# A four-layer recurrent kernel: zero rows in the head stacks, and turns for POOL's indirect transfers

## The chip, the cores and the metric

The kernel runs on one core of a Trainium2 chip. The metric is the device time of one execution in microseconds (us), and less is better. One program does everything, from the inputs in DRAM to the output in DRAM. The engines are called PE (TensorE; PEld is its weight load), DVE (VectorE), ACT (ScalarE), POOL (GpSimd) and SP (SyncE). SP computes nothing here, and issues transfers.

## The reference

`x` is `[2, 1024, 128]`, 2048 tokens of 128 numbers. Four times a layer normalisation gives `xn`, a first block gives `s` and a second one `g`:

```python
for each of four layers:
    xn = layernorm(x)
    s  = block_a(xn)
    g  = silu(block_b(xn))
    x  = x + s * g
```

Layer 0 is a differential attention with 8 heads of 2 x 128 and a feed-forward part with ternary weights. Layer 2 is a "quantum circuit" (cosines and their cumulative products) and a mixture of 16 experts that choose tokens. The change touches what serves layers 1 and 3:

```python
# layer 1, first block: 16 heads of 8 numbers, each token sees 32 to either side
scores = einsum('bhqd,bhkd->bhqk', Q, K) / sqrt(8)
scores = where(abs(i - j) <= 32, scores, -inf)
s = einsum(softmax(scores), V) @ W_o
# layer 1, second block: every token goes to one of 8 experts (the top one)
top_idx = argmax(softmax(x @ gate_w.T)); top_val = max(...) / (max(...) + 1e-8)
out = (gelu(x @ w1[top_idx]) @ w2[top_idx]) * top_val
out = layernorm(out) * ln_gamma + ln_beta
# layer 3, first block: 16 heads of 8 numbers, causal; second block: int4 weights and LoRA
```

## The kernel before, in words

The tokens are 16 tiles of 128. Each layer is a function of its own, and the layers follow each other in time: layer 0 up to about 1030 us, layer 1 from 1035 to 1350, layer 2 to 1645, layer 3 to the end.

The class `Heads` serves the attention of layers 1 and 3. `project_in` makes queries and keys, and `split3` writes each number as a sum of three bf16 parts. The parts go to DRAM (`parts`, L522), and `load_stacks` (L546, L552) brings them back as two stacks for four heads: `kk[n % 3]` (called ks in the profile) and `q[n % 3]` (qs), each `[KR, 4, S]`. Rows 0 to 71 hold products' factors, nine blocks of 8 rows, so that one bf16 matmul over 72 rows adds up all products of parts. Row maxima come first: `maxima` multiplies rows `0:KP` (72) and DVE takes the maximum (nm, L958). The negated maxima, in three bf16 parts, are then transposed and written to rows `KP:KR` (72 to 74) of qs by `maxima_rows`, where ks has ones (L491, three POOL transfers). The scores (st, L976) multiply rows `0:KR` (75), so that the maximum is subtracted inside the matmul, ACT takes the exponential (e, L1012), and `values` (o1p, L623) multiplies with v. Masks are added by a matmul of the identity with a mask in SBUF (L938, L967). A group n is four heads of one batch entry: eight groups a layer. The stacks of group n + 2 are loaded while group n is worked on, all of them from SP.

The experts of layer 1 are the class `Routed`. `route` (L649) computes each token's expert and place, and ends with 16 indirect transfers on POOL (`slots_in<-xn`, L729) that scatter the tokens into DRAM sorted by expert, 128 slots to a tile, 23 tiles (`NS1`). `steps` (L737) is a generator: per tile one indirect load of the expert's weights (`ew`, L763), which POOL issues two steps ahead, a transpose and two matmuls (L772 on), and after eight tiles the gelu and the second matmuls (`f1y`). The tokens' rows (`xs`, L748) come in three SP loads of up to 8 tiles. At the end 16 indirect loads (L835) bring the results back, one in each step, and a layer normalisation per four tiles follows.

The order of the work is written out by hand: `manual_schedule` keeps the program's order on PE, DVE, ACT and POOL. `Weave` runs two generators beside each other, here `attend(n, o)` (16 steps) and `ahead(n)`, which holds the maxima of group n + 1 and `MOE[n]` steps of the experts:

```python
MOE = (2, 8, 11, 11, 11, 11, 12, 16)
```

77 steps are to be done, and the last places of `MOE` give out a few more than are left. SP's queue has its own order, which the framework's planner makes; a transfer waits there for the eighth one before it of its kind of queue. In the first 60 us SP also writes zeros into the 23 tiles of slots (L1819) and later issues transposed tiles of layer 0 (`aT<-tT`, L292).

Of the kernel before, what the change touches and what calls it, by code (L numbers as in the profile page):

```python
# [2 lines left out]

# [1 line left out]

# [5 lines left out]
F32 = mybir.dt.float32  # L11
BF16 = mybir.dt.bfloat16
# [6 lines left out]
P = 128  # L19
B, S, D = 2, 1024, 128  # L20
NT = B * S // P
NG = NT // 4
# [7 lines left out]
E1, FF1 = 8, 256  # L30
NS1 = NT + E1 - 1
# [37 lines left out]
def rsqrt(k, pool, out, in_, n):  # L69

    k.nc.gpsimd.tensor_tensor(out, in_, k.neg_half[:, :n], ALU.pow)  # L71
# [379 lines left out]

KP, KR = 72, 75


class Heads:
# [5 lines left out]
    def __init__(self, k, ctx, weave, li, qk, v, o, bq=None, bk=None, bv=None, bo=None):  # L463
        nc, tc = k.nc, k.tc
        self.k, self.weave, self.li = k, weave, li
        self.wqk = k.wm(qk).rearrange("p (a c) -> p a c", a=2)
        self.wv, self.wo = k.wm(v), k.wm(o)
        self.bk, self.bv, self.bo = bk, bv, bo

        def pool(name, bufs, **kw):  # L470
            return ctx.enter_context(tc.tile_pool(name=f"a{li}{name}", bufs=bufs, **kw))

        self.big, self.fx, self.wk, self.ep, self.sp = (pool(n, c) for n, c in (("b", 1), ("x", 2), ("w", 2), ("e", 5 if li == 1 else 8), ("s", 3)))
        self.dr = pool("d", 1, space=bass.MemoryType.DRAM)
        self.p_s, self.p_t, self.p_o = (pool("p" + n, c, space=PSUM) for n, c in (("s", 3), ("t", 3), ("o", 2)))

        self.ident_h = self.big.tile([P, P], BF16, tag="ident_h", name=f"ident_h{li}")
        nc.vector.tensor_copy(self.ident_h, k.ident)

        self.v = self.big.tile([P, NT, H1 * self.VW + 32], F32, tag="v", name=f"v{li}")  # L480
        nc.gpsimd.memset(self.v, 1.0)
        self.scale = 1.0 / math.sqrt(DK)
        self.bq = None
        if bq is not None:
            self.bq = self.sp.tile([P, 1], F32, tag="bq", name="bq", bufs=1)
            nc.vector.tensor_scalar(self.bq, bq, self.scale, None, ALU.mult)
        self.q, self.kk = [], []
        for j in range(3):
            self.q.append(self.big.tile([KR, 4, S], BF16, tag=f"qs{j}", name=f"qs{li}{j}"))
            t = self.big.tile([KR, 4, S], BF16, tag=f"ks{j}", name=f"ks{li}{j}")  # L490
            nc.gpsimd.dma_start(  # L491
                t[KP:KR].rearrange("p h (a t) -> p (h a) t", t=P),
                k.ones_h[0 : KR - KP, None, :].to_broadcast([KR - KP, 32, P]),
            )
# [41 lines left out]
            nc.vector.tensor_tensor(dst, src, bv, ALU.add)  # L536
        yield

    def load_stacks(self, n):

        nc = self.k.nc
        b, hg = divmod(n, 4)
        heads = slice(4 * hg, 4 * hg + 4)
        d = self.parts[b]
        for a in range(3):
            nc.sync.dma_start(  # L546
                self.kk[n % 3][24 * a : 24 * a + 24], d[1].rearrange("a (d h) t -> (a d) h t", h=H1)[:, heads, :]
            )
        for a in range(3):
            for i in range(3):  # L550
                r = 24 * a + 8 * i
                nc.sync.dma_start(  # L552
                    self.q[n % 3][r : r + DK], d[0, a].rearrange("(d h) t -> d h t", h=H1)[:, heads, :]
                )

    def maxima_rows(self, n, c, nm):

# [75 lines left out]
class Routed:  # L633
# [12 lines left out]
        for _ in range(n):  # L646
            next(self.todo, None)

    def route(self):  # L649
        k, nc, pool = self.k, self.k.nc, self.pool  # L650

        def tile(name, shape, dt=F32):
# [73 lines left out]

        self.scattered = []
        for t in range(NT):
            i = nc.gpsimd.indirect_dma_start(k.slots, self.at(self.pos, t), k.xn[:, t, :], None)  # L729
            for j in self.scattered:  # L730
                k.tc.declare_no_dep(i.ins, j.ins, reason="no two tokens have the same slot")
            self.scattered.append(i)
# [5 lines left out]
    def steps(self):  # L738
# [1 line left out]
        G = 8  # L740
        xs, h, w, late = {}, {}, {}, {}

        def first(a):


            n = min(G, NS1 - a * G)
            xs[a] = pool.tile([P, G, D], F32, tag="xs", name=f"xs{a}", bufs=2)
            d = nc.sync.dma_start(  # L748
                xs[a][:, 0:n, :], k.slots[a * G * P : (a * G + n) * P, :].rearrange("(t p) d -> p t d", p=P)
            )  # L750
            for i in self.scattered:
                k.tc.add_manual_dep(
                    d.ins,
                    i.ins.name,
                    mybir.DependencyInfo(mybir.DependencyClass.Sync, mybir.DependencyReason.DATA),
                    reason="a slot's row may come from any of the scatters",
                )

        def weights(i):

            if i < NS1:
                w[i] = hd.wk.tile([P, 2 * FF1], F32, tag="ew", name=f"ew{i}", bufs=13)
                nc.gpsimd.indirect_dma_start(w[i], None, k.i["l1_w"], self.at(self.rows, i))  # L763

        def hidden(i):

            a, j = divmod(i, G)
            if i < NS1 and j == 0:
                h[a] = pool.tile([P, 2 * G + 1, P], F32, tag="h1", name=f"h1_{a}", bufs=2)
            ph = self.p.tile([P, 3, P], F32, tag="s", name=f"f1h{i}")  # L770
            if i < NS1:
                nc.tensor.transpose(ph[:, 2, :], xs[a][:, j, :], k.ident)  # L772
            if i:
                b, l = divmod(i - 1, G)
                for c in range(2):
                    nc.tensor.matmul(
                        ph[:, c, :],
                        lhsT=w[i - 1][:, c * P : (c + 1) * P],
                        rhs=h[b][:, 2 * l, :],
                        start=True,  # L780
                        stop=True,
                    )
            if i and i < NS1 and j:
                copy_on(nc, i % 2, h[a][:, 2 * j - 2 : 2 * j + 1, :], ph)
                return
            if i:
                copy_on(nc, i % 2, h[b][:, 2 * l : 2 * l + 2, :], ph[:, 0:2, :])
            if i < NS1:
                copy_on(nc, 1 - i % 2, h[a][:, 0, :], ph[:, 2, :])
# [22 lines left out]
                k.slots_out[i0 * P : (i0 + n) * P, :].rearrange("(t p) d -> p t d", p=P), y[:, 0:n, :]  # L812
            )

        first(0)
        first(1)
        for i in range(2):
            weights(i)
        yield
        for i in range(NS1 + 8):  # L820
            if i % G == G // 2 and 2 <= (i + G) // G < (NS1 + G - 1) // G:
                first((i + G) // G)
# [8 lines left out]
            for fn in late.pop(i, ()):  # L831
                fn()
            yield
        for t in range(NT):
            nc.gpsimd.indirect_dma_start(self.y[:, t, :], None, k.slots_out, self.at(self.pos, t))  # L835
# [6 lines left out]
        for n in range(NG):  # L842
# [41 lines left out]
def l1_layer(k):  # L884
    nc, tc = k.nc, k.tc
    half = WIN // 2
    with ExitStack() as ctx:
# [4 lines left out]

        def banded(name, w, step):
            m = big.tile([P, w], BF16, tag=name, name=name)
            for r in range(0, P, step):
                part = zero[r : r + step, 0:w]
                nc.gpsimd.affine_select(
                    out=part, in_=part, compare_op=ALU.is_ge, fill=-1e30, base=0, pattern=[[1, w]], channel_multiplier=-1  # L900
                )
                nc.gpsimd.affine_select(
                    out=m[r : r + step, :],
                    in_=part,
# [3 lines left out]
                    pattern=[[-1, w]],  # L908
                    channel_multiplier=1,
                )  # L910
            return m

        zero = big.tile([P, KW], F32, tag="zero", name="zero1")
        nc.gpsimd.memset(zero, 0.0)
        band = banded("band1", KW, P)
        nc.gpsimd.memset(zero, 0.0)
        inner = banded("inner1", P, P // 2)
        first = big.tile([P, P], BF16, tag="first1", name="first1b")
        last = big.tile([P, P], BF16, tag="last1", name="last1b")
        nc.gpsimd.tensor_copy(first, inner)  # L920
# [834 lines left out]
def recurrent_kernel(ctx: ExitStack, tc, ins, out, layers=(0, 1, 2, 3)):  # L1755
# [196 lines left out]
```

## Time and profile before

| what | value |
|---|---|
| median of 3 runs | 1967.15 us (1962.88 to 1970.48) |
| the profiled execution | 2018.82 us |
| its span | 2017.1 us |
| mean granted TensorE clock in it | 0.900 |
| PE busy | 1737.7 us (86%) |
| DVE busy | 1260.8 us (63%) |
| ACT busy | 829.7 us (41%) |
| POOL busy | 554.5 us (27%) |

The profile is one execution and 51.7 us longer than the median, so a length read from it is compared with its own span. In a list of groups a line reads: code line, engine, operation, output<-inputs, rows * columns of the PE array, shape, count, then busy time, mean ns, idle time before and what ended it. PEclk in the slices of the page is the granted clock in tenths. "remote" or "another core or an unknown queue" stands where no recorded instruction explains the end of a wait, and "issue" where the engine waited for nothing that the profile shows.

### The profile page before, as it was taken

Reading aid. Unit: us, or ns where it says so; the run is one execution under the profiler, and the core shown is the slowest. Engines: PE = TensorE matmul, PEld = TensorE weight load, DVE = VectorE, ACT = ScalarE, POOL = GpSimd, SP = SyncE. Lnnn points to the kernel's source line nnn. Section 1 sums busy time; section 2 is a strip of 40 time slices with the busy share of each in tenths; the row PEclk is TensorE's granted clock in tenths of the full one; section 3 lists DMA queues with packets and bytes.
Section 4 is the critical chain, followed back from the end, with each engine's and each line's share of the span. In section 5 each row is a group of like instructions: output and inputs, shape, how many; then the busy total and the mean of one; then the engine's idle time right before and its main releaser. Section 6 shows DMA issues by size and latency. Waiting matters only on the chain.

```text
span 2017.1 us, 24516 instructions
## 1 busy us (share of the span) xinstructions
PE 1737.7 (86%) x7820; PEld 894.3 (44%) x7820; DVE 1260.8 (63%) x2561; ACT 829.7 (41%) x1803; POOL 554.5 (27%) x870
## 2 busy tenths in 40 slices
PE   4999999999999999889971888765588939999996
PEld 2444444444444444334450455433366724444442
DVE  3988888888888888830032443468732464787771
ACT  2555555555555554432140344333113131566564
POOL 2333333333333333400045012111056350111201
PEclk9999999999999999999985689775689865899998
DMA  5433233333333332400015333121045233021200
GB/s 176 104 90 101 71 96 80 97 83 97 82 83 97 81 83 71 101 3 0 0 25 143 85 102 89 36 72 41 0 111 132 46 79 72 17 65 38 47 2 12
DMA packets 115504, 141.86 MB, mean 70 GB/s; under 512 B 25923, under 2 KB 100684, under 8 KB 112816
## 3 DMA queue, kind: packets, MB, share of 16 engines
q1 hardware_dynamic: 90512, 91.94, 17.7%
q0 software_dynamic: 24576, 48.33, 10.0%
q8 instruction: 63, 1.03, 0.2%
q14 instruction: 65, 0.53, 0.1%
q10 hardware_dynamic: 288, 0.03, 0.0%
HBM read 55.76 MB, written 16.78 MB: 36 GB/s over the span
## 4 chain that ended last, share of the span: by engine, by line
PE 56%; DVE 18%; DMA 7%; issue 5%; POOL 5%; ACT 4%; SPq 2%; another core or an unknown queue 1%; POOLq 0%; DVEq 0%; ACTq 0%
PE sc L261 11%; PE pz L303 6%; PE f0h L419 5%; DVE nm L271 4%; PE o3p L623 4%; DMA aT<-tT 4%; PE st L1649 3%; PE po L321 2%; DVE e L281 2%; DVE tT L285 2%; PE pq L237 2%; SPq L292 2%; POOL aT L292 2%; PE sr L1611 2%; ACT e L273 2%
## 5 line engine op out<-in xcount | busy, mean ns | idle before, releaser
L261 PE MATMUL sc<-xnT,q 128*128 128x512 f32 x1024 | 506.3, 596 | 6.4 <-ACT e L273 6.4
L273 ACT ACTIVATE e<-sc,nm 128x1024 f32<-128x1024 f32 x256 | 285.2, 1114 | 350.1 <-DVE nm L271 267.5
L271 DVE TENSOR_REDUCE nm<-sc 128x1 f32<-128x1024 f32 x256 | 307.8, 1205 | 9.1 <-PE sc L261 9.1
L261 PEld LDWEIGHTS sc<-xnT,q 128*128 128x128 f32 x1024 | 193.8, 191 | 234.1 <-issue 189.3
L292 POOL DMA_DIRECT2D aT<-tT x384 | 204.7, 540 | 322.6 <-DVE tT L285 175.1
L303 PE MATMUL pz<-aT,xn 128*128 128x512 f32 x512 | 262.1, 596 | 5.0 <-DMA aT<-tT 5.0
L1658 ACT ACTIVATE e<-st 128x512 f32<-128x512 f32 (+3 forms) x384 | 166.8, 492 | 121.9 <-PE st L1649 112.8
L281 DVE SCALAR_TENSOR_TENSOR e<-e,c,e 128x1024 f32<-128x1024 f32 x128 | 164.1, 1282 | 3.3
L285 DVE STREAM_TRANSPOSE tT<-e 128x1024 f32<-128x1024 f32 x128 | 158.4, 1238 | 2.3 <-DMA aT<-tT 1.4
L303 PEld LDWEIGHTS pz<-aT,xn 128*128 128x128 f32 x512 | 97.7, 191 | 121.1 <-issue 112.0
L71 POOL TENSOR_TENSOR f<-fv,neg_half 128x1 f32<-128x1 f32 x128 | 83.3, 651 | 201.0 <-DVE fv L335 143.4
L1619 DVE TENSOR_REDUCE nm<-sr 128x1 f32<-128x384 f32 (+3 forms) x176 | 106.4, 636 | 40.9 <-PE sr L1611 40.2
L1012 ACT ACTIVATE e<-st 128x384 f32<-128x384 f32 (+1 forms) x128 | 58.0, 476 | 171.8 <-PE st L976 146.3
L1649 PE MATMUL st<-qs,ks 75*128 75x512 bf16 (+3 forms) x384 | 117.9, 331 | 1.0 <-ACT e L1658 0.9
L321 PE MATMUL po<-vc,z 128*128 128x384 f32 x256 | 105.8, 495 | 5.6 <-ACT oc L332 2.2
L419 PE MATMUL f0h<-h,hw 128*128 128x512 f32 x256 | 110.0, 592 | 0.0
L958 DVE TENSOR_REDUCE nm<-sr 128x4 f32<-128x512 f32 x64 | 43.9, 689 | 104.5 <-PE sr L950 59.7
L1597 DVE TENSOR_REDUCE nf<-sf 128x1 f32<-128x512 f32 x128 | 82.1, 682 | 11.9 <-PE sf L1596 11.7
L623 PE MATMUL o3p<-e,v 128*32 128x512 f32 (+3 forms) x768 | 88.1, 507 | 0.0
L321 PEld LDWEIGHTS po<-vc,z 128*128 128x128 f32 x256 | 47.4, 191 | 72.6 <-issue 46.4
L433 DVE TENSOR_TENSOR f0y<-f0o,bv 128x512 f32<-128x512 f32 x4 | 2.8, 691 | 121.3 <-PE f0o L429 121.3
L237 PE MATMUL pq<-xnT,m 128*128 128x512 f32 x128 | 69.4, 624 | 7.7 <-ACT oc L332 5.6
(377 smaller groups left out, 2641.5 us busy)
## 6 DMA issues: line engine op xcount, KB each, us to landing
aT<-tT SPq DMA_DIRECT2D x640, 64.0 KB
aT<-tT POOLq DMA_DIRECT2D x384, 64.0 KB
w<-in_l_e SPq DMA_DIRECT2D x16, 768.0 KB
qs<-parts SPq DMA_DIRECT2D x144, 64.0 KB
ks<-parts SPq DMA_DIRECT2D x48, 192.0 KB
parts<-hm SPq DMA_DIRECT2D x16, 384.0 KB
w<-in_l_w POOLq DMA_DIRECT2D x8, 640.0 KB
hw<-in_l_h POOLq DMA_DIRECT2D x1, 2048.0 KB
```

What stands on the lines that cost most here:

```text
L261: nc.tensor.matmul(ps[:, n * 512 : (n + 1) * 512], lhsT=q[:, m, hf * 512 + t * P : hf * 512 + (t + 1) * P], rhs=k.xnT[:, b * S + n * 512 : ...
L271: nc.vector.tensor_reduce(nm, ps, AX.X, ALU.max, negate=True)
L273: nc.scalar.activation(em, ps, AF.Exp, bias=nm, accum_out=(s1, s2)[m][:, t : t + 1])
L281: nc.vector.scalar_tensor_tensor(e[0], e[1], c, e[0], ALU.mult, ALU.add)
L285: nc.vector.transpose(tT[:, :, t % 2, :, :].rearrange("p j J c -> p J j c"), e[0].rearrange("p (J j a) -> p J j a", J=8, j=4),)
L292: (nc.gpsimd if j == 3 or (i == 0 and j > 0) else nc.sync).dma_start(aT[32 * j : 32 * j + 32, t - 1 : t + 1, i, :, :].rearrange("a t J c - ...
L303: nc.tensor.matmul(pz, lhsT=k.xn[:, 8 * b + J, :], rhs=st["aT"][:, :, :, J, :].rearrange("p t i c -> p (t i) c"), start=(J == 0), stop=(J ...
L321: nc.tensor.matmul(po.rearrange("p a d -> p (a d)"), lhsT=st["z"][:, t * P : (t + 1) * P], rhs=mats[h][1].rearrange("p a d -> p (a d)"), s ...
L419: nc.tensor.matmul(ph, lhsT=hw[:, l, c, j * P : (j + 1) * P], rhs=cur[:, c, cols], start=(c == 0), stop=(c == 3))
L623: nc.tensor.matmul(po[32 * i : 32 * i + 32, c0:c1], lhsT=self.v[:, kt, vc : vc + 32], rhs=es[i], start=start, stop=stop, skip_group_check= ...
L1649: nc.tensor.matmul(ps[:, n0:512], lhsT=kk[0:KR, i, kt * P : (kt + 1) * P], rhs=q[0:KR, i, c * 512 + n0 : c * 512 + 512], start=not diag, s ...
L1658: nc.scalar.activation(e[:, n0:512], ps[:, n0:512], AF.Exp)
```

## The change

The stacks have 128 rows instead of 75. The maxima contract rows 0 to 95 and the scores all 128: rows 72 to 95 and 99 to 127 are zeros on both sides, the three rows of maxima (ones in ks) become 96 to 98. A DRAM buffer `blank` holds these 56 rows; three SP transfers at the program's start fill it, and in layers 1 and 3 six SP transfers copy it into the three ks and the three qs.

In layer 1 the 16 scatters alternate with other work of POOL: building the band mask, and the 12 loads of the stacks of group 2, which SP issued before. The routing moves into the hand-ordered part. The rows of a slot tile come by a plain POOL load behind each indirect one of weights, four steps ahead. The gathers come in four groups of four, and the next group is issued behind the reciprocal root of the group before. The number of steps goes from 77 to 61, and `MOE` changes with it; `e` has 6 buffers instead of 5, `ew` 14 instead of 13.

```diff
-KP, KR = 72, 75
+KD, KP, KM, KR = 72, 96, 99, P
...
-            nc.gpsimd.dma_start(
-                t[KP:KR].rearrange("p h (a t) -> p (h a) t", t=P),
-                k.ones_h[0 : KR - KP, None, :].to_broadcast([KR - KP, 32, P]),
-            )
+            for x in (t, q):
+                nc.sync.dma_start(x[KD:P].rearrange("p h t -> p (h t)"), k.blank)
+            self.q.append(q)
...
-    def load_stacks(self, n):
+    def load_stacks(self, n, eng=None):
+        for _ in self.loading_stacks(n, eng or self.k.nc.sync):
+            pass
...
         for t in range(NT):
+            if t:
+                next(between)
             i = nc.gpsimd.indirect_dma_start(k.slots, self.at(self.pos, t), k.xn[:, t, :], None)
...
+        def load(i):
+            if i >= NS1:
+                return
+            w[i] = hd.wk.tile([P, 2 * FF1], F32, tag="ew", name=f"ew{i}", bufs=14)
+            nc.gpsimd.indirect_dma_start(w[i], None, k.i["l1_w"], self.at(self.rows, i))
+            xs[i] = hd.wk.tile([P, D], F32, tag="xs", name=f"xs{i}", bufs=6)
+            d = nc.gpsimd.dma_start(xs[i], k.slots[i * P : (i + 1) * P, :])
+            for x in self.scattered:
+                k.tc.add_manual_dep(
...
-        first(0)
-        first(1)
-        for i in range(2):
-            weights(i)
+        for i in range(4):
+            load(i)
         yield
-        for i in range(NS1 + 8):
...
-            weights(i + 2)
+        for i in range(NS1 + 6):
+            load(i + 4)
...
-        for t in range(NT):
-            nc.gpsimd.indirect_dma_start(self.y[:, t, :], None, k.slots_out, self.at(self.pos, t))
-            yield
-        for _ in range(3):
+        def gather(n):
+            for t in range(4 * n, 4 * n + 4):
+                nc.gpsimd.indirect_dma_start(self.y[:, t, :], None, k.slots_out, self.at(self.pos, t))
+
+        gather(0)
+        for _ in range(5):
             yield
...
             rsqrt(k, hd.wk, rs, ve, 4)
+            if n + 1 < NG:
+                gather(n + 1)
             yield
...
-        MOE = (2, 8, 11, 11, 11, 11, 12, 16)
+        MOE = (0, 8, 10, 10, 10, 12, 12, 16)
...
-            if n + 2 < 8:
+            if 2 < n + 2 < 8:
                 hd.load_stacks(n + 2)
...
-        moe.route()
         with tc.manual_schedule(engines={E.PE, E.DVE, E.Activation, E.Pool}):
+            moe.route(chain(banding(band, KW, P), hd.loading_stacks(2, nc.gpsimd)))
...
+    k.blank = dp.tile([P - KD, 4 * S], BF16, tag="blank", name="blank")
+    fill = cp.tile([P, D], BF16, tag="fill", name="fill")
+    nc.gpsimd.memset(fill, 0.0)
+    blank = k.blank.rearrange("r (a t) -> r a t", t=D)
+    for r0, r1, x in ((KD, KP, fill), (KP, KM, k.ones_h), (KM, P, fill)):
+        nc.sync.dma_start(blank[r0 - KD : r1 - KD], x[0 : r1 - r0, None, :].to_broadcast([r1 - r0, 4 * S // D, D]))
```

More of the change, by code (lines that the diff above doesn't have):

```diff
@@ L2 @@
 from contextlib import ExitStack
+from itertools import chain
 import numpy as np
@@ L471, in pool @@
             return ctx.enter_context(tc.tile_pool(name=f"a{li}{name}", bufs=bufs, **kw))
-        self.big, self.fx, self.wk, self.ep, self.sp = (pool(n, c) for n, c in (("b", 1), ("x", 2), ("w", 2), ("e", 5 if li == 1 else 8), ("s", 3)))
+        self.big, self.fx, self.wk, self.ep, self.sp = (pool(n, c) for n, c in (("b", 1), ("x", 2), ("w", 2), ("e", 6 if li == 1 else 8), ("s", 3)))
         self.dr = pool("d", 1, space=bass.MemoryType.DRAM)
@@ L488, in __init__ @@
         for j in range(3):
-            self.q.append(self.big.tile([KR, 4, S], BF16, tag=f"qs{j}", name=f"qs{li}{j}"))
+            q = self.big.tile([KR, 4, S], BF16, tag=f"qs{j}", name=f"qs{li}{j}")
             t = self.big.tile([KR, 4, S], BF16, tag=f"ks{j}", name=f"ks{li}{j}")
-            nc.gpsimd.dma_start(
-                t[KP:KR].rearrange("p h (a t) -> p (h a) t", t=P),
-                k.ones_h[0 : KR - KP, None, :].to_broadcast([KR - KP, 32, P]),
-            )
+            for x in (t, q):
+                nc.sync.dma_start(x[KD:P].rearrange("p h t -> p (h t)"), k.blank)
+            self.q.append(q)
             self.kk.append(t)
@@ L537, in project_in, with loading_stacks @@
         yield
-    def load_stacks(self, n):
-        nc = self.k.nc
+    def load_stacks(self, n, eng=None):
+        for _ in self.loading_stacks(n, eng or self.k.nc.sync):
+            pass
+    def loading_stacks(self, n, eng):
         b, hg = divmod(n, 4)
@@ L545, in load_stacks @@
         for a in range(3):
-            nc.sync.dma_start(
+            eng.dma_start(
                 self.kk[n % 3][24 * a : 24 * a + 24], d[1].rearrange("a (d h) t -> (a d) h t", h=H1)[:, heads, :]
             )
+            yield
         for a in range(3):
@@ L551, in load_stacks @@
                 r = 24 * a + 8 * i
-                nc.sync.dma_start(
+                eng.dma_start(
                     self.q[n % 3][r : r + DK], d[0, a].rearrange("(d h) t -> d h t", h=H1)[:, heads, :]
                 )
+                yield
     def maxima_rows(self, n, c, nm):
@@ L647, in step, with route @@
             next(self.todo, None)
-    def route(self):
+    def route(self, between):
         k, nc, pool = self.k, self.k.nc, self.pool
@@ L741, in steps @@
         xs, h, w, late = {}, {}, {}, {}
[L743 to L751, printed above, removed]
+        def load(i):
[6 more added lines that the diff above has]
+            for x in self.scattered:
                 k.tc.add_manual_dep(
                     d.ins,
-                    i.ins.name,
+                    x.ins.name,
                     mybir.DependencyInfo(mybir.DependencyClass.Sync, mybir.DependencyReason.DATA),
@@ L757, in first @@
                 )
[L759 to L763, printed above, removed]
         def hidden(i):
@@ L771, in hidden @@
             if i < NS1:
-                nc.tensor.transpose(ph[:, 2, :], xs[a][:, j, :], k.ident)
+                nc.tensor.transpose(ph[:, 2, :], xs[i], k.ident)
             if i:
@@ L813, in second @@
             )
-        first(0)
-        first(1)
-        for i in range(2):
-            weights(i)
+        for i in range(4):
+            load(i)
         yield
-        for i in range(NS1 + 8):
-            if i % G == G // 2 and 2 <= (i + G) // G < (NS1 + G - 1) // G:
-                first((i + G) // G)
-            weights(i + 2)
+        for i in range(NS1 + 6):
+            load(i + 4)
             if i <= NS1:
@@ L890, in l1_layer, with banding @@
         big, p_s, p_t, p_o, ep, sp = hd.big, hd.p_s, hd.p_t, hd.p_o, hd.ep, hd.sp
-        def banded(name, w, step):
-            m = big.tile([P, w], BF16, tag=name, name=name)
+        def banding(m, w, step):
+            nc.gpsimd.memset(zero, 0.0)
+            yield
             for r in range(0, P, step):
@@ L901, in banded @@
                 )
+                yield
                 nc.gpsimd.affine_select(
@@ L910, in banded @@
                 )
-            return m
+                yield
         zero = big.tile([P, KW], F32, tag="zero", name="zero1")
[L914 to L917, printed above, removed]
+        band = big.tile([P, KW], BF16, tag="band1", name="band1")
+        inner = big.tile([P, P], BF16, tag="inner1", name="inner1")
+        for _ in banding(inner, P, P // 2):
+            pass
         first = big.tile([P, P], BF16, tag="first1", name="first1b")
```

## The prediction

> **What bounds the kernel now.** I read the slices of the page, the chain of waits in the two stretches that the change touches (layer 1: 1040–1110 and 1250–1273 us; layer 3's entry), the engines' timelines there, and a table of windows with the granted clock.
>
> ```profile
> span 2017.1 us, 24516 instructions
> PE   4999999999999999889971888765588939999996
> PEclk9999999999999999999985689775689865899998
> ```
>
> TensorE is busy 86% of the span, and layer 0 (to 1030 us) keeps it full at full clock. From slice 21 on (1008 us) the clock row goes down to 5 to 8 though the busy row often says 8 or 9 (slice 34: clock 5, busy 9): a busy TensorE there may be one at half clock. Windows (start:end, length, then busy us of PE, PEld, DVE, ACT, POOL, then clock):
>
> ```profile
> 1116.81:1137.31 20.50, 20.50 (x152) 9.18 (x149) 7.25 (x17) 5.21 (x12) 0.00 (x0) 0.50 0.47 92
> 1284.50:1300.70 16.20, 16.20 (x217) 9.40 (x216) 10.66 (x32) 7.08 (x17) 0.14 (x1) 1.00 0.37 77
> 1304.56:1321.63 17.07, 17.07 (x133) 8.29 (x129) 11.40 (x33) 4.82 (x10) 1.02 (x1) 0.50 0.01 2
> 1553.73:1557.15 3.42, 3.40 (x9) 1.13 (x8) 0.61 (x2) 1.78 (x3) 2.43 (x2) 1.00 0.67 214
> ```
>
> For 20.5 us TensorE is never idle and has half its clock; the same kind of work in the second line has the full one. The first line's groups of short matmuls are
>
> ```profile
> L976 PE MATMUL st<-qs,ks 75*128 75x192 bf16 x20 | 5.3, 367 | 0.0
> L950 PE MATMUL sr<-ks,qs 72*64 72x128 bf16 x48 | 4.2, 314 | 0.0
> ```
>
> so about half of the time goes to matmuls of 72 or 75 rows. The second thing in layer 1 is stalls that no engine of the kernel explains. From the chain:
>
> ```profile
> 1082.92 4.96 another core or an unknown queue
> 1088.60 9.79 another core or an unknown queue
> 1100.04 6.11 another core or an unknown queue
> ...
> 1253.87 4.31 issue
> ```
>
> and from the timelines of DVE, PE and POOL (last bracket: idle before, and who ended it):
>
> ```profile
> 1271.66 1.29 DVE L958 TENSOR_REDUCE nm<-sr 128x4 f32<-128x512 f32 x2 [14.91 <-remote]
> 1263.20 0.21 PE L623 MATMUL o1p<-e,v 128*32 128x32 f32 x1 [0.75 <-issue]
> 1264.60 0.21 PE L623 MATMUL o1p<-e,v 128*32 128x32 f32 x1 [1.19 <-issue]
> 1266.42 0.94 POOL L835 DMA_INDIRECT xnT<-slots_out,posi  x1 [0.30 <-issue]
> ```
>
> While POOL issues indirect transfers back to back, one every 1.25 us (28 in 1066–1102, 16 in 1249–1269), DVE, ACT and PE creep: DVE waits for a reduction's input that was complete, and PE does one 0.21 us matmul per 1.4 us. In layer 2, where pairs of indirects alternate with waits for DVE, DVE and PE don't creep.
>
> **The change, part by part.** The profiled execution is 2018.8 us, 51.7 above the median of 1967.15. The sum below is made on the profiled one first.
>
> *1. Rows filled: 72→96 in the maxima, 75→128 in the scores.* Columns, and so the streaming time at one clock, stay; no instruction is added on PE. What can change is the clock. By windows of about 3.41 us (the spacing of the clock's steps) I weighed the streaming time with rows/128, columns streamed at 2.4 per ns at full clock (sc's 512 fp32 columns, two passes, repeat every 0.429 us). In 1116.8–1133.9 the share is 0.63–0.71 and the clock stays at half; in 1133.9–1137.3, with the 128-row projections, it is 0.89 and the clock rises. Elsewhere 0.76 left it low and 0.80 raised it. And in the line at 1553.73 PE is 3.40 of 3.42 us busy, mostly with h2p of 16 rows, and the clock falls right after. [...] I take rows. With 96 and 128 rows the same windows become 0.72–0.81, and the one before, 1113.4, 0.78. So the rise should come some five windows earlier. Gains, at half the time spent there less what DVE and ACT then bound: 1116.8–1137.3: 10.2 at most, 8 taken; 1147.5–1154.4 (0.75): 3.4 at most, 2.5; 1308–1321.6 (0.81): 6.8 at most, 5.5; layer 3, one window at 1724.4 (0.75 to 0.92): 1.7. In layer 3's 1700–1720 DVE is busy 19.3 of 19.5 us and the share stays under 0.72: nothing. Sum −18 (bounds 0 and −22).
>
> *2. Blanks: six SP transfers of 0.46 MB per layer (2.75 MB) for three POOL ones.* At 154–323 GB/s, which slices of the DMA view of 1040–1110 reach, 2.75 MB take 8.5–18 us. Layer 1: they can start at about 1034 and end by 1043–1052; the last parts land at 1062 and sr starts at 1077.5, so hidden; uncovered they would cost up to 6. Layer 3: stacks are first needed at 1697 and were there at 1676; hidden by FFN matmuls (L1744, L1745), 20 us of slack. In layer 3 POOL's three issues stood on the chain:
>
> ```profile
> 1654.19 0.76 POOL ks L491
> ...
> 1656.25 1.30 POOL ks L491 x2
> ```
>
> so −2. In layer 1 they are off it: 0. SP waits eight DMAs back on its own lanes; behind the blanks stand only parts and stacks.
>
> *3. The start.* Three SP transfers write the blank (0.46 MB in 256 B runs) ahead of the zeros:
>
> ```profile
> 6.04 21.40 SPq L1819 DMA_DIRECT2D slots_in<-zeros  x23
> 56.66 3.37 SPq L292 DMA_DIRECT2D aT<-tT  x5
> ```
>
> Issue 3 × 0.93 us (21.4/23). The third moves 29 rows. [...] no run of before has such a shape. Then 237.6 KB run on one engine: at a sixteenth of the 351 GB/s of 5–10 us, 11 us; at 63 ns a packet (q1: 90512 packets in 17.7% of 16 × 2017 us), 928 packets take 58. The first aT issue on SP is at 56.7 and its reader at 77.7. Every DMA waits for the eighth before it on its kind of queue, so the eighth zero waits for the slow one, and 15 more (14 us) follow: aT's issue at about 22 + T us for a transfer of T. With the 15 us that lie between aT's landing and its reader, nothing is late below T of about 50. I take +2 (0 to +18).
>
> *4. Scatters take turns* with a memset, two mask selects, 3 ks and 9 qs loads, moved from SP to POOL. In the changed order each scatter (0.97 us) has one of these behind it; those loads are wanted by maxima of group 2, and the band mask by the first scores, after maxima of group 0, so 15 more slots of 0.6–1 us are covered. SP loses 12 issues of 0.3–0.4 us in group 0: off the path. What follows on POOL (ew, xs) comes some 10 us later, but steps 0 to 8 of the experts now begin in group 1 instead of 0 (MOE 2→0), so that is covered too.
>
> *5. Experts' rows* come as 23 POOL loads of 64 KB between the ew's instead of three SP loads. A step then needs about 1.25 + 0.6 us of POOL against at least 1.5 us of a step on PE; four steps ahead (6 us) against 3 to 5 of landing (the stacks' 5.9). The first xs waits for the last scatter's landing, some 3 us, with only ew's and xs's queued behind it. Buffers of ew go from 13 to 14, of xs 6, of e 5 to 6: 0.
>
> *6. Gathers in fours*, each after the statistics of the four before (DVE). The waiting POOL has nothing queued behind but those. The wait costs a group at most one gather's latency, 4 × 1.25 + 3, under six weave steps. The count of steps drops from 77 to 61 and nothing is left for group 7, which took 20 us with 11 steps to do: −4 (−8 to 0).
>
> *7. The stalls* (profiled): 4.96 + 9.79 + 6.11 = 20.9 at the first series; some 4 at the 8 ew's of 1187–1202; about 16 at the gather (14.9 on DVE). Sum 40, less a remainder of 2: −38.
>
> Profiled: −18 − 2 + 2 − 4 − 38 = −60, so 2018.8 → about 1959. For the median it matters whether the stalls are there without the profiler. 40 us of stalls plus about 5 of clock lost in them is nearly all of the 51.7 us of excess, and layer 0, where PE streams at its own pace, leaves the excess no room. So I take them as the profiler's own and count only −18 − 2 − 4 + 2 = −22.
>
> **The rivals.**
>
> A, likeliest (0.50): as worked out, 1945; own range 1930–1957.
>
> B (0.22): the stalls are real. For: they look like hardware behaviour around POOL's series, and the excess may sit elsewhere. Against: the match of sums. Then 35–38 more: about 1908 (1895–1925).
>
> C (0.13): neither part bites. The clock follows time, or zeros in the rows don't count for it, or the shares of 0.72–0.81 are too near the edge (0.76–0.80); and the turns, in the profile, leave the stalls. Then −2 − 4 + 2: about 1962.
>
> D (0.15), the other side: the 29 rows on one engine. The start is late by T − 50 (above). To lose over 0.5% (10 us) net of the 22 gained, 32 us are needed: T = 82 to 84, 90 ns per 256 B run against the queue's mean of 63. (The same 0.46 MB also stand in front of layer 0's w, which lands at 29.0 on the chain.) The queue's mean is of larger packets, which speaks against it. It decides from 90 ns; at 120 ns (T = 111) it gives about 1945 + 61 = 2006, at 100 about 1945 + 43 = 1988.
>
> **How the numbers follow.** A measurement of this kernel can tell about 0.5% from no change: 1957.3 and 1977.0. A is 0.47 faster and 0.03 same; B 0.22 faster; C 0.03 faster, 0.08 same, 0.02 slower; D 0.02 faster (mild), 0.01 same, 0.12 slower. That makes 0.74, 0.12 and 0.14. The range 1900–1976 leaves out D's slower part and the low end of B (0.03); C's upper tail adds little.
>
> **What would show it.** In the profile after: span near 1957; first waits of nm in layer 1 under 2 us and POOL's scatters with DMAs between; the first exp of group 0 near 1094 instead of 1113.7, and PEclk 1.00 from a window after it (group 0 in 22 us, not 30); st 128 rows; PE gone from half clock near the end of group 6; aT's first SP issue near 57. Wrong: clock still 0.50 in busy stretches of 96/128 rows (C); nm still waits for a remote releaser (C); profiled and median dropping alike (B); first aT after 60 and a later first pz (D).

## The result and the profile after

The changed kernel takes 1949.76 us (median of 7, 1937.71 to 1953.26), the kernel before 1967.15 (7 runs, 1960.71 to 1972.0). The ratio is 0.990 with a 95% interval of 0.9876 to 0.9923: faster, by about 17 to 20 us. 1945 was forecast, within 1900 to 1976. The profiled execution fell by 81 us, from 2018.8 to 1937.7, and it is now the lowest of the seven runs. That difference between 81 and 17 is the first thing to explain. The page after (span, PE and granted clock by slices):

```profile
span 1936.0 us, 24573 instructions
PE   4999999999999999989996788865588839999995
PEclk9999999999999999999997799876698966999998
```

Where the clock row had 5, 6, 8, 9, 7, 7 in slices 22 to 27 it now has 7, 7, 9, 9, 8, 7. Layer 1, group 0 of the heads, first the window (columns as in the windows of before), then two groups of matmuls in it:

```profile
1082.80:1102.40 19.60, 19.60 (x209) 10.51 (x209) 9.47 (x21) 8.37 (x18) 15.99 (x21) 0.85 0.31 96
```

```profile
L982 PE MATMUL st<-qs,ks 128*128 128x192 bf16 x24 | 4.3, 266 | 0.0
L956 PE MATMUL sr<-ks,qs 96*64 96x128 bf16 x56 | 4.0, 257 | 0.0
```

The same matmuls, with 75 and 72 rows, ran at 367 and 314 ns in the window of before with the clock at 0.50; now they take 266 and 257 on the mean of a window at 0.85. The first exp stands at 1082.8, 11 us ahead of the 1094 that was looked for. POOL is busy for 16 of the 19.6 us and nobody waits for it. DVE's waits at the scatters (engine, what it waited for; us in total, times, longest):

```profile
DVE nm L964 <- PE sr L956: 18.9, 15, 5.1
```

No "remote" is left, but the longest wait is 5.1 us, where the prediction looked for less than 2. At the gathers POOL's timeline shows the fours, each behind a DVE wait:

```profile
1213.69 0.95 POOL L835 DMA_INDIRECT xnT<-slots_out,posi  x1 [0.30 <-issue]
1218.64 1.05 POOL L72 TENSOR_TENSOR rs<-ve,neg_half 128x4 f32<-128x4 f32 x1 [4.00 <-DVE ve L852]
1219.89 1.00 POOL L835 DMA_INDIRECT xnT<-slots_out,posi  x1 [0.19 <-issue]
```

Layer 1, from its first xn to its last exp, went from 310.5 us to 242.2. The start did not suffer: the first aT issue on SP stands at 58.3.

### The profile page after: what moved, and what is told of

Same layout as the page of the kernel before. It is cut to its first block, busy times and chain, and to the rows that moved or that the text cites. A ratio compares the mean times of both kernels' runs of the same rounds, so it can differ in the third digit from the quotient of the medians.

```text
span 1936.0 us, 24573 instructions
## 1 busy us (share of the span) xinstructions
PE 1700.2 (88%) x7820; PEld 873.7 (45%) x7820; DVE 1260.3 (65%) x2561; ACT 830.1 (43%) x1803; POOL 574.4 (30%) x900
## 4 chain that ended last, share of the span: by engine, by line
PE 54%; DVE 20%; DMA 9%; POOL 5%; issue 5%; ACT 4%; SPq 3%; POOLq 0%; DVEq 0%; ACTq 0%
PE sc L262 12%; PE pz L304 6%; PE f0h L420 6%; DVE nm L272 4%; PE o3p L628 4%; DMA aT<-tT 4%; PE st L1655 3%; PE po L322 2%; DVE e L282 2%; SPq L293 2%; DVE tT L286 2%; PE pq L238 2%; PE sr L1617 2%; POOL aT L293 2%; ACT e L274 2%
## 5 line engine op out<-in xcount | busy, mean ns | idle before, releaser
L1655 PE MATMUL st<-qs,ks 128*128 128x512 bf16 (+3 forms) x384 | 116.7, 329 | 1.0 <-ACT e L1664 0.9
L420 PEld LDWEIGHTS f0h<-h,hw 128*128 128x128 f32 x256 | 48.6, 190 | 61.2 <-issue 61.2
```

What stands on the lines that cost most here:

```text
L420: nc.tensor.matmul(ph, lhsT=hw[:, l, c, j * P : (j + 1) * P], rhs=cur[:, c, cols], start=(c == 0), stop=(c == 3))
L1655: nc.tensor.matmul(ps[:, n0:512], lhsT=kk[0:KR, i, kt * P : (kt + 1) * P], rhs=q[0:KR, i, c * 512 + n0 : c * 512 + 512], start=not diag, s ...
```

## The experiments

The runs come from four chips, here A to D, and "before there" is the kernel before on the same chip. "Layer 1" is the stretch from the first xn to the last exp of the profiled execution, "loop 3" the stretch from the first exp to the last in layer 3, group 0 the time from its first exp to that of group 1.

| run | chip | median, us | before there | ratio (95%) | layer 1 | group 0 | loop 3 |
|---|---|---|---|---|---|---|---|
| before, page shown | ? | | | | 310.5 | 29.8 | 284.7 |
| e5 before again | B | 1963.0 (one) | 1968.0 | | 255.6 | 32.5 | 284.7 |
| e1 blank | A | 1958.8 | 1966.5 | 0.996 (0.9942–0.9979) | 257.9 | 35.8 | 287.5 |
| e2 fill | A | 1952.8 | 1966.5 | 0.9933 (0.9908–0.9958) | 248.4 | 35.4 | 282.0 |
| e3 turns | A | 1966.8 | 1966.5 | 0.9997 (0.9974–1.002) | 254.8 | 27.2 | 286.2 |
| e4 changed kernel | A | 1939.7 | 1966.5 | 0.988 (0.9843–0.9918) | 239.9 | 20.8 | 280.8 |
| e6 series | B | 1961.5 | 1968.0 | 0.9977 (0.9962–0.9993) | 260.1 | 30.9 | 284.4 |
| e7 fill, no step in group 0 | B | 1966.8 | 1968.0 | 0.9987 (0.997–1.0003) | 260.7 | 21.2 | 282.5 |
| e8 gathers in series | B | 1955.8 | 1968.0 | 0.9937 (0.9916–0.9959) | 252.7 | 21.4 | 282.6 |
| e9 fill, stacks 2 on POOL | C | 1988.0 | 2015.7 | 0.9859 (0.9833–0.9885) | 282.7 | 30.7 | 282.0 |
| e10 changed + lora rows | C | 1937.8 | 2015.7 | 0.9617 (0.9591–0.9642) | 248.9 | 21.6 | 280.0 |
| e11 turns again | C | 1975.2 (one) | 2015.7 | | 261.6 | 27.3 | 286.2 |
| e12 as e10 | D | 1936.3 | 1971.0 | 0.9832 (0.9808–0.9856) | 242.2 | 20.7 | 281.4 |

Two stretches differ between executions of the same code, and a difference between two kernels that is no larger proves nothing. Group 6 of layer 1, with 72 and 75 rows, takes 20.4 us at clock 1.00 in e5 and 26.0 us at 0.67 in e6, though both run the layer 1 of before. Layer 3 from its seventh matmul of qp (the projection of queries and keys) to its first exp takes 63.8 us in e4 and 56.3 in the profile after, which is the same kernel.

### Rows and turns apart (e1 to e4)

The first takes before and only brings the ones rows in the new way:

```diff
-KP, KR = 72, 75
+KD, KP, KM, KR = 72, 72, 75, 75
...
-            nc.gpsimd.dma_start(t[KP:KR]..., k.ones_h[0 : KR - KP, None, :]...)
+            for x in (t, q):
+                nc.sync.dma_start(x[KD:P].rearrange("p h t -> p (h t)"), k.blank)
```

> The kernel before with only the way changed in which the ones rows come: six SP transfers of the blank per head layer for POOL's three; the matmuls contract 72 and 75 rows as before, POOL's series stand as before. The maxima rows stay at 72 to 74. In the planned order of DVE the last parts of the keys now stand ahead of the routing's first reduction. Theory (mine, formed after the result): the entry of layer 1 is then some 8 to 10 us shorter and layer 3's some 2, so the median falls by about 11 us to 1956, and the profiled execution falls by about the same from 2019 to 2007, with all its stalls (nm waits of 5 to 10 us, 15 us at the gather) in place. Rival: the entry is hidden again by something later, median within 3 us of before.

Measured: 1958.8, 8 us less where 11 were forecast; but the profiled execution is 1963.4, not 2007, and none of the long waits is in it, though POOL issues the same 28 and 16 transfers. The order of DVE changed as said, and the entry of layer 1 (first xn to first exp) takes 49.5 us against 57.6 in e5. But layer 1 as a whole is no shorter (257.9 against 255.6). Group 0 is 3.3 us longer, where PE waits 4.9 us for xs at f1h, the transpose of the first tile of slots, against 1.8 in e5. Groups 1, 3 and 6 are 1.4, 1.7 and 3.9 longer with the same instructions at a lower clock (0.79 against 1.00 in group 6). So what lowers the median isn't seen in these two profiles.

The second adds the rows: `KD, KP, KM, KR = 72, 96, 99, P`.

> As the first, plus 96 and 128 rows contracted; POOL's series as before. Theory that rows move the clock: against the first run another 10 to 18 us, so a median of 1938 to 1946, and in the profile st and sr of groups 0, 1 and 6 at PEclk 1.00 a few windows after they start, stalls in place, profiled about 1990. Rival (the clock follows busy time alone): equal to the first run within 3 us.

Measured: 6 us less than e1 in the median, 9.5 less in layer 1 and 5.5 in loop 3. That is less than the 10 to 18 of the rows' theory and more than the 3 of its rival. Of the 9.5, 5.6 lie in groups 3 and 6, and e5 runs these just as fast with 72 and 75 rows (25.8 and 20.4 us), so they cannot be given to the rows. What differs clearly is the clock of group 0: it is full 2.7 us after the first exp in e2, and 31.4 us after it in e1. Why so little of that shows in the length of group 0: the waits of e2 there, then e1's, then the two windows of the group, e1's and e2's:

```profile
DVE xf L514 <- PE qp L507: 15.7, 1, 15.7
ACT h L64 <- PE f1h L771: 12.7, 1, 12.7
...
PE f1h L771 <- DMA xs<-slots_in: 12.3, 1, 12.3
```

```profile
PE f1h L771 <- DMA xs<-slots_in: 4.9, 1, 4.9
```

```profile
1085.40:1121.20 35.80, 29.75 (x217) 14.08 (x217) 11.21 (x23) 10.41 (x22) 12.82 (x14) 0.56 0.67 163
```

```profile
1084.50:1119.90 35.40, 21.58 (x217) 11.60 (x217) 11.17 (x23) 10.44 (x23) 11.85 (x13) 0.77 0.70 165
```

The filled rows save 8.2 us of PE in the same 217 matmuls (29.75 to 21.58, clock 0.56 to 0.77), and 7.4 of them go into a longer wait for xs, which is in place at 1111.0 in e1 and 1109.9 in e2. SP issued xs at 1092.6 (1093.2 in e1), behind the 12 loads of group 2's stacks, so I read xs as late for that, which is argued and not shown; e9 moves those loads.

The third is the changed kernel with the rows of before (`KD, KP, KM, KR = 72, 72, 75, 75`).

> The changed kernel with 72 and 75 rows contracted (maxima rows at 72 to 74), everything else of the change in place. Theory that the stalls belong to the profiled execution: median only 2 to 6 us under the first run (1950 to 1954), while the profiled execution is 40 us or more under that of the first run (about 1960). Rival (stalls are real): the median too is 35 to 40 us under that of the first run, about 1918; but then the changed kernel itself could not stand at 1950.

Measured: 1966.8, no gain at all, 8 us above e1. Its profiled execution agrees with the other runs, and the 40 us that were to separate it from e1's aren't there, since e1 has no stalls either.

> The changed kernel again, beside the three others on one chip: 1950 in the median and 1938 profiled, as on record. If rows and turns add up, its distance to the first run is the sum of those of the second and third; if turns cost time in the plain run, it lies above the second.

Measured: 1939.7 (6 runs; on record were 1949.8). From e3 to e4 the rows alone are worth 27 us by the medians, and 14.9 in layer 1 plus 5.4 in loop 3 by the profiles. The safer figure is that of the profiles, about 20: the changed kernel's own two medians, 1939.7 here and 1949.8 on record, lie 10 us apart. Group 0 in e3 and in e4:

```profile
1086.90:1114.10 27.20, 25.68 (x216) 12.78 (x216) 11.32 (x23) 10.04 (x21) 19.49 (x25) 0.67 0.40 115
```

```profile
1084.80:1105.50 20.70, 19.24 (x216) 10.70 (x216) 11.05 (x23) 9.89 (x21) 16.77 (x22) 0.93 0.36 106
```

Rows and turns do not add up: with the turns the wait for xs is gone, group 0 runs through, and what the clock gives is kept. e11 repeats e3's group 0 (27.3), and e8, e10 and e12 repeat e4's (20.7 to 21.6).

### Whose stalls? (e5, e6)

> The kernel before, unchanged, one more profiled execution. The first two runs had POOL's series of 28 and 16 indirect transfers as before, and their profiled executions show none of the long waits. Theory that the 40 us of stalls belonged to one execution (whatever held it): the span is about 1965, exp of group 0 starts near 1085 to 1093, no wait of nm over 6 us at the scatters and none over 3 at the gather. Rival (they come with this program whenever it is profiled): span about 2017 and the waits of 5, 10, 6 and 15 us are there again.

Measured: span 1961.3. The waits at the scatters and at the gathers, each from the same stretch as those of the page shown before:

```profile
DVE nm L958 <- PE sr L950: 27.5, 13, 12.0
...
DVE nm L958 <- PE sr L950: 5.8, 8, 1.2
```

A releaser is known for each, and the wait of 14.9 us is 1.2 at most. The one of 12.0 is above the 6 of the forecast, but it is DVE's first wait for maxima, and PE itself waits there for the stacks (`qs<-parts`, 14.8 us). POOL's 16 gathers take the same 944 ns each in both executions. So the stalls do not come with profiling this program.

```diff
...
+        for i in range(NPROBE):
+            y = tmp.tile([P, D], F32, tag="probe", name=f"probe{i}", bufs=8)
+            nc.gpsimd.indirect_dma_start(y, None, k.slots, bass.IndirectOffsetOnAxis(ap=rows[:, 0:1], axis=0))
...
+NPROBE = 64
```

> The kernel before with 64 more indirect loads (128 rows of 512 B, from the slots buffer, into a tile that nothing reads) issued back to back on POOL beside layer 0's feed-forward part, where POOL is idle for 142 us and PE streams. Theory that a series does no harm: the time stays within 4 us of before, and PE's stretch from 878 to 1030 keeps its length; POOL shows about one load every 1.25 us. Rival (a series slows DVE, ACT and PE, 40 us for the 44 transfers of layer 1): 50 us or more longer, in the profile or in both.

Measured: 1961.5, not longer; and PE beside the series:

```profile
905.00:1000.00 95.00, 95.00 (x222) 41.99 (x221) 1.06 (x3) 19.83 (x28) 60.55 (x64) 1.00 0.15 44
```

64 transfers in a row, 60.6 us of POOL, and the 222 matmuls keep their 95.00 us, as they do in the same window of the page shown before. On this chip a series is harmless. Its ratio of 0.9977 for pure addition also says how far two different programs can lie apart for no reason that I can name: some 5 us.

### Which part of the turns? (e7, e8, e9)

The seventh is e2 with `MOE = (0, 9, 11, 11, 11, 12, 12, 16)`.

> The second run (filled rows, POOL's series as before) with the experts' steps shared out as (0, 9, 11, 11, 11, 12, 12, 16) instead of (2, 8, 11, 11, 11, 11, 12, 16): no step in group 0. Theory: what the turns gave on top of the filled rows is mostly that PE no longer stands in group 0 before the first transposed tile (f1h waits 12.3 us there for xs, whose load waits for the last scatter): 5 to 10 us less than the second run's 1952.8, about 1945, and group 0 takes 23 to 28 us instead of 35. Rival (the turns themselves gave it): as the second run, within 3 us.

Measured: group 0 falls to 21.2 us as expected, but the ratio is 0.9987 where e2 had 0.9933, some 11 us worse. The wait moved instead of going:

```profile
DVE nm L957 <- PE sr L949: 20.1, 6, 17.1
PEld f1h L771 <- issue: 15.0, 2, 14.8
PE f1h L771 <- DMA xs<-slots_in: 14.6, 1, 14.6
```

Now SP has issued xs only at 1117.8, behind the stacks of group 3 too, and group 1 takes 44.7 us against 29.0 in e2. Sharing the steps out differently does not help as long as SP loads these rows behind the stacks.

The eighth issues all 16 gathers where the changed kernel issues the first four.

> The changed kernel with all 16 gathers issued in one series when the first group is due, instead of fours that wait for DVE; the 61 steps stay. Theory that a series does no harm: 1945 to 1950, as the changed kernel, within its interval. Rival (a series of gathers stalls the engines): 10 to 15 us longer, with nm, e or matmul waits of over 5 us without a releaser in the stretch of the gathers.

Measured: 1955.8, ratio 0.9937 against 0.988 and 0.990 of the changed kernel, and 12.8 us more in layer 1 than e4, of which 10.6 lie in group 5 (32.3 against 21.7). It is the rival's number with another mechanism:

```profile
1231.42 0.17 DVE L857 TENSOR_TENSOR rs<-rs,tv 128x4 f32<-128x4 f32 x1 [12.06 <-POOL rs L72]
```

No engine creeps. The reciprocal root `rs` stands on POOL behind the 12 further gathers, so DVE waits 12 us for it, and PE and ACT wait for DVE. The fours have their use even where a series harms nobody: they let `rs` in.

The ninth is e2 with group 2's stacks loaded from POOL behind the scatters:

```diff
-                hd.load_stacks(n + 2)
+                hd.load_stacks(n + 2, None if n else nc.gpsimd)
```

> The second run (filled rows, POOL's series as before) with one thing of the turns alone: the 12 loads of group 2's stacks go from SP to POOL, behind the 16 scatters. Theory: what the turns gave on top of the filled rows lies in SP's queue and the transfers there, where xs (512 KB each) was issued at 1092.6 behind these 12 loads, landed with them and let PE wait 12.3 us at f1h in group 0. Then that wait is under 3 us here, group 0 takes about 25 us instead of 35, and the median is 5 to 10 us under the second run's 1952.8. Rival (xs was late for another reason, the scatters or the bandwidth): the wait stays, and the median within 3 us of it.

Measured: PE reaches its first f1h without a wait. But the chip, C, has the kernel before at 2015.7 (9 runs, 2007.5 to 2017.8), so the median can't be set beside e2's, and the stalls are back. They decide the test: they hold PE off the first f1h until 1121.1, 25.3 us after SP issued xs, where e2 had xs 17.3 us after the issue. So whether the stacks had made xs late stays open. The profiled execution took 1992.6, the longest of five runs that begin at 1981.5, so the others can't be without most of these waits:

```profile
DVE nm L958 <- remote: 39.3, 6, 14.9
ACT e L1012 <- remote: 33.7, 4, 12.2
```

```profile
1249.54 1.29 DVE L958 TENSOR_REDUCE nm<-sr 128x4 f32<-128x512 f32 x2 [14.95 <-remote]
1243.20 0.21 PE L623 MATMUL o1p<-e,v 128*32 128x32 f32 x1 [1.83 <-issue]
```

The first two lines are waits of 1060–1280, the others from DVE's and PE's timelines: the same 14.9 us and the same single matmuls as in the page shown of before.

### Another short stack filled (e10 to e12)

```diff
-    k.lora_b = cp.tile([RANK + 1, D], F32, tag="lora_b", name="lora_b")
-    nc.gpsimd.dma_start(k.lora_b, ins["l3_b"])
+    k.lora_b = cp.tile([P, D], F32, tag="lora_b", name="lora_b")
+    nc.vector.memset(k.lora_b, 0.0)
+    nc.gpsimd.dma_start(k.lora_b[0 : RANK + 1], ins["l3_b"])
...
-        zT = pool.tile([RANK + 1, 512], F32, tag="zT", name=f"zT{n}", bufs=2)
+        zT = pool.tile([P, 512], F32, tag="zT", name=f"zT{n}", bufs=2)
```

> The changed kernel with one more stack of rows filled: in layer 3 the 32 small matmuls f3y<-lora_b,zT contract 128 rows (lora_b zero below row 17, zT ones there) instead of 17. No instruction and no column is added. In the changed kernel's profile PE is busy 57.7 of the 62 us 1593-1655 at half clock throughout, with 12.7 us in these matmuls. Theory that rows move the clock: PEclk 1.00 from about two windows after the first f3y on, this stretch 10 to 20 us shorter, median about 1933. Rival (the clock follows busy time): no change of the stretch, median as the changed kernel, 1940 to 1950.

Layer 3's entry, from its seventh matmul of qp to the first exp, in e4: the window, and two groups (counted over 1593–1655):

```profile
1581.70:1645.50 63.80, 53.88 (x166) 27.55 (x165) 31.30 (x65) 13.23 (x25) 12.18 (x19) 0.54 0.57 123
```

```profile
L1751 PE MATMUL f3y<-lora_b,zT 17*128 17x128 f32 x32 | 12.7, 497 | 0.0
L1750 PE MATMUL f3y<-wq,xnT 128*128 128x128 f32 x32 | 12.6, 497 | 0.0
```

And in e10 (groups over 1593–1640):

```profile
1590.30:1639.20 48.90, 36.60 (x166) 19.35 (x165) 31.34 (x65) 13.27 (x26) 11.84 (x19) 0.69 0.71 159
```

```profile
L1751 PE MATMUL f3y<-lora_b,zT 128*128 128x128 f32 x32 | 7.0, 304 | 0.2 <-DVE zT L1746 0.2
L1750 PE MATMUL f3y<-wq,xnT 128*128 128x128 f32 x32 | 7.0, 303 | 0.0
```

The same 166 matmuls take 36.6 us of PE instead of 53.9. Not only the filled matmuls are faster but their untouched neighbours too (497 to 303 ns). Nearly all of that is the clock's: in the profile after, with 17 rows, both groups take 482 to 497 ns where the clock is 0.50 (1595–1602 us) and 323 to 326 where it is 1.00 (1605.2–1611). PE was busy 53.9 of 63.8 us in e4 (84%), at a clock of 0.54, and 36.6 of 48.9 in e10 (75%), at 0.69: the clock rose where the busy share fell. The stretch, at 0.69 and not at 1.00, gains 15 us against e4 and 7 against the profile after (56.3). The filled matmuls f3y and their neighbours take 7.0 us each here, 12.7 and 12.6 in e4, 9.1 and 9.5 in the profile after, 11.4 and 11.3 in the page shown of before.

> The third run's kernel once more, for its stages: its median stood 8 us above the first run's, though its layer 1 (from the first xn to the last exp) took 254.8 us against 257.9 there. If the loss lies in layer 1, this one takes 260 or more; if it lies behind layer 1, where both kernels have the same order of instructions, it is the clock's luck in those stages, and layer 1 again takes about 255.

Measured: layer 1 took 261.6, on chip C, where one "remote" wait of 2.4 us was left. That chip and this question can't be separated, so why e3's median lies 8 us above e1's stays open. Behind layer 1 both executions of the turns take 674.4 us against 667.8 in e1, with the same order of instructions.

> The kernel of the tenth run once more. That run's chip had the kernel before at 2015.7, 48 us over the other two chips, so its 1937.8 can't be set against the changed kernel's 1940 to 1950 there. Theory that the filled rows of f3y move the clock in layer 3's entry (48.9 us from qp to the first exp there, against 56 to 64 in the changed kernel's two profiles): on a chip with the kernel before at 1967 the median is 1928 to 1940, a ratio of 0.978 to 0.986, and that stretch takes about 50 us again. Rival (luck of that chip): the ratio is the changed kernel's 0.988 to 0.990, and the stretch takes 56 to 64 us. If the chip is one with the kernel before at 2015, the ratio is 0.96 again.

Measured on chip D: 1936.3, ratio 0.9832 (0.9808–0.9856), the stretch 49.3 us with 36.6 us of PE at a clock of 0.69, as in e10. The interval lies below that of the changed kernel on record (0.9876–0.9923) and overlaps a little with e4's (0.9843–0.9918). So this version beats the kernel before clearly. That its whole time beats the changed kernel's is not shown: 1936.3 is 13 us under the median on record, but only 3 under e4's, each on another chip.

## Why the prediction was right, and where it wasn't

The forecast of 1945 was met, and the largest term, the rows, for its own reason. That the sum fits so well is partly luck: the shorter entry and the end of the wait for xs were not in it, and the −4 of the tail did not come.

**Rows (step 1, −18): right in its cause; that the sum fits is in part luck.** With the turns in place (e3 to e4) the rows took 14.9 us off layer 1 and 5.4 off loop 3, some 20 together. But the terms were 8, 2.5 and 5.5 for groups 0, 1 and 6 and 1.7 for layer 3, and they came out as 6.5, 5.9, 0 and 5.4. Group 6 takes 23.6 us in e3 and in e4; without the turns its half clock comes and goes between executions of the same code (0.67 in the page of before and in e6, 1.00 in e5). The cause is clearest in group 0. In all eight traces with filled rows the clock is full 2.7 to 6.0 us after the first exp; in the six with 72 and 75 rows it takes 18.2 to 31.4 us. Loop 3 too divides by rows: 280.0 to 282.6 us with them filled, 284.4 to 287.5 without. That the clock went with the rows here and not with busy time is shown again by e10, where PE's busy share fell from 84% to 75% and the clock rose from 0.54 to 0.69. Whether the edge lies at a share of 0.76 to 0.80, as the step read it from one page, no run tested. The rows themselves cost no time: at a clock of 1.00 two score matmuls of 192 columns take 0.33 us with 75 rows (before, L976 at 1286.4) and 0.33 with 128 (after, L982 at 1088.8). The step's 2.4 columns per ns, with f32 columns counted twice, stands in before at the same clock: 177 f0h matmuls of 512 f32 columns take 75.96 us (0.429 each), 128 f0o of 128 f32 columns 14.31 (0.112 each), and four sr of 128 bf16 columns 0.22 (L1602 at 1737.1, 0.055 each).

**Blanks (step 2): hidden, but the entry term was missed.** The blank copies hide as said. Removing POOL's ones from layer 1 was put at 0, "off it", for the chain. Yet the planner then placed the last parts of the keys ahead of the routing's reduction, and the entry became 8 us shorter (57.6 to 49.5). It is a term of the sum that was mis-sized: −8 at the entry, of which some 3 are lost again at f1h in e1, where xs comes over SP. The −2 in layer 3 can't be seen: from qp to the first exp it is 62.6 and 62.9 before, 60.7, 63.7 and 63.6 in e1 to e3.

**Start (step 3, +2; rival D): 0.** SP's zeros took 35.4 us instead of 21.4, so the blank did hold the queue by some 14 us; but aT is issued at 58.3, as at 58.4 in e5. What held the queue was not the eighth zero's wait, as the step had it, but the issue of the first zero, which alone takes 24.5 us in the trace after (no zero's takes over 0.8 in before). The cause was the piece of 29 rows, as D had it: in the trace after, its packets of 256 bytes run until 35.4 us, and from 29.6 to 33.6 us DMA moves only 18 GB/s, at a share of 0.08 (one of 16 engines is 0.06). That such a piece would run on one engine no trace of before had shown. In e1 and e3, whose pieces have 3, 48 and 5 rows, they end by 15.7 us, and the zeros take 18.0 and 18.2 us. Issued at 6.9, the piece needed a T of about 28, far from the 50 from which aT would be late.

**Scatters' turns and the experts' rows (steps 4 and 5, 0): their use was missed.** They take the loads of group 2 off SP and xs with them; which of the two ends the wait for xs was not separated. Without them, a wait of 4.9 to 12.3 us at f1h eats what was gained before it (e1, e2), or moves (e7). In the page shown of before this wait did not matter, for the stalls hid it, and in e5 it is 1.8 us.

**Gathers and the tail (step 6, −4): right for group 7, not for the sum.** Group 7 went from 19.2 us in e2 to 13.2. But groups 5 and 6, which took over steps, got 5.6 and 3.3 longer, so the three together are 3 us longer and not 4 shorter. Over groups 1 to 7 e4 is 5.7 us longer than e2; its gain lies in group 0 (20.7 against 35.4). What the fours are worth against one series is the 10.6 us of group 5 (e8), for `rs` on POOL, which the step did not name.

**Stalls (step 7): the number for the median was right, and its reason wrong.** The step took 40 us of stalls "as the profiler's own", because with some lost clock they matched the excess of 51.7. What failed is that step from a matching sum to a cause. The runs show the stalls in the trace of e9 on chip C, where the kernel before takes 2015.7 in the median of 9, and none in the traces of A and B (before: 1966.5, 1968.0). The page's 2018.8 fits a chip like C; on which one it was taken is not known. So rival B was true on one chip of four, as far as e9 stands for the kernel before, which was not profiled there: on C the kernels with turns took 1937.8 and 1975.2, without a wait like those, and e9 with its series 1988.0. The profiled sum of −60 came out at −81, mostly since layer 1 without stalls is 255.6 and not 310.5: 55 us, where 38 to 45 were counted.

## What to carry to other kernels

Where PE is fully busy at half clock, look at the rows of its matmuls: zero or one rows that cost no column can raise the clock for the neighbours as well (e10: 0.54 to 0.69 over the stretch, the neighbours from 497 to 303 ns). A gain on one engine is kept only if the next transfer it meets is early enough, so follow the queue of that transfer before you count the gain. A profile is one execution on one chip: if it lies 2.6% above the median, profile the same kernel again, before any of its waits is given a cause.

## What the runs showed of the hardware that I had not expected

One chip of four runs the kernel before 45 to 49 us slower than the others (2015.7 against 1966.5 to 1971.0). While POOL issues indirect transfers back to back there (e9), DVE, ACT and PE wait up to 14.9 us for data that no recorded instruction holds back; in the traces of A and B the same series, with the same 0.94 us per transfer every 1.25, disturbs nobody. What differs on that chip was not found, and the series of 64 was not run there.

Ones multiplied by zeros counted for the clock too: in e10 the filled part of zT holds ones and that of lora_b zeros, and the clock of the stretch was 0.69 against 0.54 in e4. In the stacks the added rows are zeros on both sides, and the clock of group 0 went from 0.56 (e1) to 0.77 (e2).
